# A bias product as a 129th matmul column, a softplus split in two for PE to add, and a new list of steps, in a four-layer graph network kernel

## The chip, the cores and the metric

The kernel runs on one core of one Trainium2 chip. The metric is the device time of one execution in microseconds (us); the median of several runs counts. Profiles come from one further execution, whose own time is given beside its span. Engines: PE multiplies matrices, DVE is VectorE, ACT is ScalarE, POOL is GpSimd, SP issues most transfers.

## What is computed

128 graphs of 64 nodes with 128 features pass through four layers, each of the form x = x + layer(relu(layernorm(x)), adj). The two that the change touches:

```python
# layer 0
g = exp(coeff * (e[..., None] - offsets) ** 2)      # e = adj, 64 offsets
Wf = (ssp(g @ W1.T + b1) @ W2.T + b2) * adj * adj
y = einsum('bjf,bijf->bif', r @ Wa.T, Wf)
y = ssp(y @ Wd1.T + bd1) @ Wd2.T + bd2              # ssp(x) = softplus(x) - log 2
# layer 1 (hyperbolic)
h = proj(mobius_matvec(W, x))                       # uses |x|, |mx| with mx = x @ W.T
h = proj(mobius_add(h, hyp_bias))                   # uses sum(h * hyp_bias) per node
# ... attention over neighbours with silu and a sigmoid, an MLP, expmap, logmap
```

Layer 2 is a convolution with the normalised adjacency, layer 3 a mean of messages. About a quarter of the entries of adj are not zero.

## The kernel before

Eight graphs form a group (NP = 4 pairs; a pair's 128 nodes are the partitions), and there are 16 groups. A node tile is 128 x 4 x 128, that is 128 x 512 values. Neighbours are kept as lists of slots in three blocks (512, 512 and 208 columns), so a neighbour's work comes as tiles of 128 x 1024 or 128 x 512 and their 208-column rests.

Each part of a group's work is a generator called a stream: `load`, `order` (the neighbour lists), `normed_x`, `layer0` with `weights_of`, `squares`, `duo`, `filter_of` and `neighbours`, `layer1_nodes`, `layer1_edges` with `coefs_of`, `rows`, `scores_of` and `heads`, `rest1`, `rest2`, and a few that prepare weights. Each `yield on(engine, ...)` begins a step, which issues a few instructions. The global order is a string written out in full, `ORDER` (492 steps for one iteration). An entry `name@-k` lets that stream of the group k iterations behind do its next step; `name@=k` does a step once, in iteration k. `Weave.run` walks the list for every iteration, so several groups are in flight, and each engine executes its instructions in just the order in which the list issued them. `Weave` also counts the buffers: a step that names a ring takes one of its buffers, `release` gives it back, and `shared(name, 2)` gives it back after two users. In PSUM the ring "big" has three buffers of 128 x 2 x 512 and "sm" two of 128 x 512.

```python
        for name_ in takes:
            used = self.rings[name_][1]
            s.tokens.setdefault(name_, []).append(len(used))
            used.append(False)
```

When a step asks for ACT's other table (`table="log"` or `"silu"`), a table load is issued first (L923); there are five per group in the steady part.

In `layer1_nodes`, layer 0 ends: Wd1 product (L1729 to L1733), ACT copies it with its bias from PSUM (L1737), DVE clamps it at 40 into a second tile (L1740), ACT takes Exp and Ln(1 + .) of that (L1743, L1744), DVE takes the maximum of the two tiles (L1747), and the Wd2 product follows in the helper `pairs_mm` (L1240). Layer 1 begins: x1 (L1755), layernorm (`bn` L1267; `normed` from L1302 on, once per group), transposes (L1233), an ACT copy (L1207), and the linear product, again at L1240. `product_with_bias` multiplies that product by the hyperbolic bias on POOL (L1789) and sums over features on DVE (`reduce_d`, L1259) into `mhb`, four numbers per node row, read at L1690 and L1864.

Other lines that the prediction names. Layer 0, edges: squared weights (L1584, ACT), gaussians (L1600, L1603, ACT), W1 product (L1617) and its Exp and Ln (L1624, L1627), W2 product (L1634) and its product with neighbours (L1639, DVE; L1398 adds halves), the neighbour product (L1663) and ACT's copy (L1669); L1483 scales Wa's product on ACT. Layer 1, edges: spread coefficients (L1385, L1388, L2079, DVE), their products (L2094, L2098, PE), SiLU (L2103, ACT), the score product (L2120, PE), Tanh into a row (L2126, ACT), which goes out and comes back by DMA as th and is put in its place at L2059 (DVE); L2181 follows PE's L2179, and L1319 (`sc`) is a root on ACT. Layer 1, nodes: L1705 to L1719, L1851 to L1868. Layer 2: v (L1282, ACT, the normalised x) enters the adjacency product (L1254, PE, tiles adjT and v); L1433 is the sort key of `order`; L2265, L1287 and L2272 are layer 1's last step on ACT.

Of the kernel before, what the change touches and what calls it, by code (L numbers as in the profile page):

```python
# [20 lines left out]
NP = 4  # L21
GROUPS = B // (2 * NP)
P = 128
# [741 lines left out]
SOFT_MAX = 40.0  # L765
# [10 lines left out]
heads20@-4 turned_from5@=2 heads20@-4 duo00@-2 rest2@-5 layer1_nodes@-3 rest2@-5 filter_of00@-2  # L776
duo02@-2 rest2@-5 product_with_bias@-3 rest2@-5 slots_ranks@=-2 coefs_of12@-4 weights_of12@-2
coefs_of12@-4 product_with_bias@-3 layer1_nodes@-3 coefs_of12@-4 weights2@=3 neighbours00@-2
rest2@-5 filter_of01@-2 turned_from0@=-4 layer1_nodes@-3 duo02@-2 filter_of00@-2 neighbours00@-2
filter_of00@-2 filter_of01@-2 slots_ranks@=0 weights0@=-2 coefs_of20@-4 layer1_nodes@-3  # L780
coefs_of20@-4 layer1_nodes@-3 layer1_edges@-4 layer1_edges@-4 layer1_nodes@-3 layer1_nodes@-3
weights1@=-5 layer1_edges@-4 layer1_nodes@-3 layer1_nodes@-3 rest1@-4 weights2@=3 layer1_nodes@-3
rest1@-4 layer1_nodes@-3 turned_from1@=-2 rest1@-4 layer1_nodes@-3 neighbours01@-2 filter_of02@-2
rest1@-4 filter_of00@-2 layer1_nodes@-3 neighbours01@-2 filter_of02@-2 filter_of01@-2 squares10@-2
layer1_nodes@-3 rest2@-5 layer1_nodes@-3 layer1_nodes@-3 turned_from2@=0 order@-1 layer1_nodes@-3
layer1_nodes@-3 layer1_nodes@-3 layer1_nodes@-3 layer1_nodes@-3 rest1@-4 layer0@-2 layer1_nodes@-3
order@-1 layer1_nodes@-3 layer1_nodes@-3 rest1@-4 layer1_nodes@-3 layer1_nodes@-3 rest2@-5
layer1_nodes@-3 layer1_nodes@-3 layer1_nodes@-3 layer1_nodes@-3 layer1_nodes@-3 layer1_nodes@-3
filter_of00@-2 layer1_nodes@-3 layer1_nodes@-3 layer1_nodes@-3 layer1_nodes@-3 layer1_nodes@-3
turned_from5@=2 layer1_nodes@-3 filter_of00@-2 layer1_nodes@-3 layer1_nodes@-3 norm_of_sum@-3  # L790
neighbours02@-2 duo20@-2 rest2@-5 weights0@=1 filter_of01@-2 rest2@-5 weights0@=1 filter_of00@-2
filter_of00@-2 filter_of01@-2 norm_of_sum@-3 rest2@-5 filter_of02@-2 neighbours02@-2 duo20@-2
layer1_nodes@-3 duo20@-2 rest2@-5 norm_of_sum@-3 layer1_nodes@-3 layer1_nodes@-3 layer1_nodes@-3
order@-1 filter_of01@-2 rest2@-5 filter_of01@-2 weights2@=2 filter_of03@-2 neighbours03@-2
weights2@=2 rest1@-4 layer1_nodes@-3 weights0@=1 filter_of03@-2 neighbours03@-2 rest1@-4
layer1_nodes@-3 filter_of03@-2 layer1_nodes@-3 squares20@-2 filter_of02@-2 order@-1 norm_of_h@-3
x_self@-4 rest2@-5 filter_of02@-2 weights0@=1 filter_of01@-2 norm_of_h@-3 filter_of02@-2
filter_of02@-2 duo22@-2 weights0@=1 layer1_nodes@-3 filter_of20@-2 duo22@-2 layer1_nodes@-3
duo22@-2 filter_of20@-2 layer1_nodes@-3 layer1_nodes@-3 order@-1 layer1_nodes@-3 filter_of02@-2
neighbours20@-2 filter_of22@-2 attention@-3 neighbours20@-2 layer1_nodes@-3 filter_of20@-2  # L800
weights2@=2 layer1_nodes@-3 order@-1 rest2@-5 layer1_nodes@-3 order@-1 layer1_nodes@-3
layer1_nodes@-3 weights0@=1 rest2@-5 attention@-3 filter_of22@-2 layer1_nodes@-3 filter_of22@-2
filter_of03@-2 turned_from1@=-4 filter_of20@-2 order@-1 duo10@-2 one_minus_z@-3 weights0@=0
one_minus_z@-3 rest2@-5 filter_of03@-2 one_minus_z@-3 layer1_nodes@-3 filter_of03@-2
filter_of03@-2 turned_from0@=-2 one_minus_z@-3 layer1_nodes@-3 order@-1 duo10@-2 one_minus_z@-3
rest2@-5 filter_of03@-2 filter_of20@-2 order@-1 filter_of20@-2 layer1_nodes@-3 layer1_nodes@-3
slots_ranks@=-5 layer1_nodes@-3 layer1_nodes@-3 layer1_nodes@-3 layer1_nodes@-3 layer1_nodes@-3
layer1_nodes@-3 layer1_nodes@-3 layer1_nodes@-3 layer1_nodes@-3 layer1_nodes@-3 order@-1
attention@-3 neighbours22@-2 turned_from3@=-2 order@-1 duo10@-2 rest2@-5 attention@-3
neighbours22@-2 order@-1 duo12@-2 weights2@=2 turned_from4@=1 filter_of10@-2 rest2@-5  # L810
filter_of11@-2 duo12@-2 filter_of10@-2 rest2@-5 filter_of10@-2 order@-1 filter_of11@-2
neighbours10@-2 filter_of22@-2 weights0@=-2 rest2@-5 layer1_nodes@-3 rest2@-5 neighbours10@-2
filter_of10@-2 rest2@-5 order@-1 filter_of22@-2 layer1_nodes@-3 filter_of22@-2 filter_of10@-2
duo12@-2 layer1_nodes@-3 rest2@-5 filter_of11@-2 rest2@-5 filter_of12@-2 neighbours11@-2 order@-1
filter_of11@-2 layer1_nodes@-3 layer1_nodes@-3 turned_from3@=-2 layer1_nodes@-3 weights1@=0
filter_of12@-2 neighbours11@-2 filter_of12@-2 squares12@-2 filter_of10@-2 rest2@-5 weights2@=2
filter_of10@-2 layer1_nodes@-3 filter_of10@-2 layer1_edges@-3 coefs_of02@-3 order@-1
filter_of11@-2 order@-1 rest2@-5 filter_of11@-2 coefs_of00@-3 order@-1 rest1@-4 rest2@-5
filter_of13@-2 neighbours12@-2 neighbours13@-2 filter_of13@-2 neighbours12@-2 filter_of13@-2
neighbours13@-2 filter_of12@-2 rows00@-3 filter_of13@-2 turned_from4@=1 order@-1 rest2@-5  # L820
filter_of11@-2 filter_of12@-2 layer0@-2 rows00@-3 filter_of11@-2 filter_of12@-2 filter_of13@-2
filter_of12@-2 filter_of13@-2 filter_of12@-2 rest1@-4 rest1@-4 rows02@-3 scores_of00@-3
scores_of01@-3 rest1@-4 filter_of13@-2 rows02@-3 weights0@=-2 filter_of13@-2 layer0@-2 normed_x@-1
rest1@-4 scores_of00@-3 scores_of01@-3 sums_of_columns@-1 no_scores@-3 product_with_h@-4 rest1@-4
normed_x@-1 normed_x@-1 normed_x@-1 product_with_h@-4 coefs_of10@-3 product_with_h@-4 rest1@-4
scores_of02@-3 heads00@-3 scores_of03@-3 normed_x@-1 rows10@-3 rest1@-4 heads00@-3 normed_x@-1
scores_of02@-3 rest1@-4 rest1@-4 rest1@-4 rest1@-4 rest1@-4 rest1@-4 rest1@-4 rest1@-4 weights1@=1
rest1@-4 rest1@-4 rest1@-4 rest1@-4 order@-1 rest1@-4 rest1@-4 order@-1 coefs_of12@-3 rows10@-3
normed_x@-1 weights0@=-2 layer1_nodes@-2 normed_x@-1 scores_of03@-3 sum_of_both@-4 layer1_nodes@-2
heads02@-3 rows12@-3 scores_of10@-3 scores_of11@-3 rest1@-4 rest1@-4 rest1@-4 coefs_of20@-3  # L830
weights0@=-2 rest1@-4 coefs_of00@-3 rest1@-4 layer1_nodes@-2 rest1@-4 rows12@-3 rest1@-4 rest1@-4
coefs_of00@-3 rest1@-4 rest1@-4 rest1@-4 weights0@=-1 order@-1 rest1@-4 layer1_edges@-3 heads02@-3
layer1_nodes@-2 scores_of10@-3 scores_of11@-3 rest1@-4 layer1_nodes@-2 rest1@-4 order@-1 rest1@-4
order@-1 coefs_of00@-3 layer0@-1 rest1@-4 coefs_of02@-3 rest1@-4 weights_of00@-1 rest1@-4
scores_of12@-3 layer1_nodes@-2 heads10@-3 duo00@-1 weights2@=2 scores_of13@-3 weights0@=-2 load@0
coefs_of02@-3 rest1@-4 layer1_nodes@-2 rest1@-4 coefs_of00@-3 rest1@-4 coefs_of02@-3 rest1@-4
rest1@-4 rest1@-4 layer1_nodes@-2 weights2@=2 rest1@-4 sum_of_both@-4 coefs_of02@-3
weights_of02@-1 scores_of12@-3 heads10@-3 squares00@-1 duo00@-1 scores_of13@-3 weights1@=-3
rest1@-4 rest1@-4 layer1_nodes@-2 rest1@-4 rows22@-3 rows20@-3 turned_from2@=-2 heads12@-3
heads12@-3 squares02@-1 rest1@-4 rows22@-3 layer1_nodes@-2 layer1_nodes@-2 rows20@-3 coefs_of10@-3  # L840
rest1@-4 rest1@-4 coefs_of10@-3 rest1@-4 coefs_of10@-3 rest1@-4 rest2@-4 scores_of22@-3
layer1_nodes@-2 scores_of22@-3 layer1_nodes@-2 norm_of_h1@-2 scores_of20@-3 layer1_nodes@-2
root_of_sums@-4 rest2@-4 layer1_nodes@-2 scores_of20@-3 layer1_nodes@-2 coefs_of12@-3
coefs_of10@-3 weights_of10@-1 weights_of20@-1 rest2@-4 layer1_nodes@-2 weights0@=-1 duo02@-1
"""


def elements(ap):
    n = 1
    for d in ap.shape[1:]:  # L850
        n *= d
    return n


class Stream:
# [92 lines left out]
def sparse_stack(ctx: ExitStack, tc: tile.TileContext, ins, out: bass.AP, flag):  # L948
# [103 lines left out]
    def matrix(name):  # L1052
        return const.tile([P, P], F32, name=name)
# [44 lines left out]
    def weights0():  # L1098
# [19 lines left out]
        yield from turned(raw["Wd1"], wd1T)  # L1118
        w.event("weights0")

    wlinT, attT = matrix("wlinT"), const.tile([P, 2 * P], F32, name="attT")
    m1aT, m1bT, m2T = (matrix(n) for n in ("m1aT", "m1bT", "m2T"))
    hab2, aw2 = (const.tile([P, 1], F32, name=n) for n in ("hab2", "aw2"))
    aw2b = const.tile([P, 32], F32, name="aw2b")
# [1329 lines left out]
```

## Time and profile before

| | before |
|---|---|
| median of 3 runs | 1788.97 us (1787.3 to 1789.33) |
| profiled execution | 1789.83 us, its span 1788.0 us |
| PE busy | 1580.1 us (88%), 10231 instructions |
| DVE busy | 1576.3 us (88%), 4872 |
| ACT busy | 1496.0 us (84%), 2784; of it 92 table loads of 1.28 us |
| POOL busy | 413.3 us (23%), 717 |
| L1302, once per group, starts at | 113.2, 204.3, 301.7, then about every 102 us to 1626.6 |

Busy time counts an engine's own instructions; the span is that of the profiled execution, and its own time is 1.83 us longer. "PEclk" in a window is the TensorE clock that was granted, 1.00 being full speed. In a group's row, "x16" counts instances, then come busy time, mean duration in ns, and the idle time of the engine just before with what ended it. The chain of waits is followed back from the end of a window: each row is a stretch in which the named instructions decided when the next could begin. The product of four small matmuls is listed as x8, since each is issued as two instructions.

### The profile page before, as it was taken

How to read it: one execution, taken by the hardware profiler on the slowest of the kernel's cores; microseconds unless marked ns; L12 is line 12 of the kernel's file. 1: busy time of each engine (PE TensorE's matmuls, PEld its weight loads, DVE VectorE, ACT ScalarE, POOL GpSimd, SP SyncE). 2: the span in 40 equal slices, each digit the busy share in tenths (PEclk: the TensorE clock that was granted, in tenths of full speed). 3: DMA queues.
4: the chain of work that ended last, by engine and by line, in shares of the span. 5: the costliest groups of instructions: out<-in, count | busy, mean ns of one | idle time of the engine just before them, and what ended most of it. 6: DMA issues, size and time to landing. Idle time of an engine off the chain costs nothing.

```text
span 1788.0 us, 30233 instructions
## 1 busy us (share of the span) xinstructions
PE 1580.1 (88%) x10231; PEld 855.9 (48%) x10231; DVE 1576.3 (88%) x4872; ACT 1496.0 (84%) x2784; POOL 413.3 (23%) x717
## 2 busy tenths in 40 slices
PE   3969888998989899898989899898989989896853
PEld 2424444545545455454545454554545455454542
DVE  5659799999999999999999999999999999988853
ACT  2858898989899898989899898989989898986632
POOL 1010113123221413223121312322141322302221
PEclk8979999999999999999999999999999999997865
DMA  2000202011110202011020201111020201102110
GB/s 62 6 1 7 57 7 54 11 43 24 27 46 16 58 7 57 17 34 34 16 58 10 60 10 38 30 27 46 16 58 1 50 18 29 36 7 58 33 37 9
DMA packets 57173, 54.22 MB, mean 30 GB/s; under 512 B 13616, under 2 KB 40624, under 8 KB 57008
## 3 DMA queue, kind: packets, MB, share of 16 engines
q1 hardware_dynamic: 57008, 52.19, 11.8%
q8 instruction: 83, 1.36, 0.3%
q14 instruction: 82, 0.67, 0.1%
HBM read 7.61 MB, written 4.19 MB: 7 GB/s over the span
## 4 chain that ended last, share of the span: by engine, by line
PE 48%; ACT 30%; DVE 14%; issue 3%; POOL 2%; DMA 2%; SPq 1%; DVEq 0%; ACTq 0%; POOLq 0%
PE big L1634 7%; PE sm L1240 7%; PE big L2094 6%; PE big L2076 5%; PE big L1617 5%; PE big L1663 4%; ACT ex L1624 4%; PE sm L2120 3%; ACT ex L1627 3%; PE big L2098 3%; ACT e L1600 3%; DVE ex L1639 2%; ACT ra L1669 2%; ACT e L1603 2%; PE sm L1247 2%
## 5 line engine op out<-in xcount | busy, mean ns | idle before, releaser
L1634 PE MATMUL big<-ex,w2T 128*128 128x512 f32 (+1 forms) x768 | 296.5, 519 | 10.4 <-DVE den L1707 5.6
L1639 DVE SCALAR_TENSOR_TENSOR ex<-big,c_L_gnn_b,ra 128x1024 f32<-128x1024 f32 (+1 forms) x160 | 198.4, 1240 | 28.4 <-PE big L1634 27.0
L1617 PE MATMUL big<-e,w1T 64*128 64x512 f32 (+1 forms) x768 | 187.2, 581 | 10.9 <-ACT e L1603 8.3
L1634 PEld LDWEIGHTS big<-ex,w2T 128*128 128x128 f32 x768 | 134.2, 190 | 122.2 <-issue 72.5
L1624 ACT ACTIVATE ex<-big,c_L_gnn_b 128x1024 f32<-128x1024 f32 (+1 forms) x160 | 174.5, 1091 | 7.4 <-PE big L1617 6.9
L2094 PE MATMUL big<-va,U 64*128 64x512 f32 (+1 forms) x768 | 175.3, 532 | 4.9 <-DVE va L2079 4.9
L1663 PE MATMUL big<-va,a 64*128 64x512 f32 (+1 forms) x768 | 176.8, 560 | 2.9 <-ACT va L1584 1.8
L2103 ACT ACTIVATE ex<-big,c_L_gnn_att_b 128x1024 f32<-128x1024 f32 (+1 forms) x160 | 167.6, 1078 | 9.8 <-PE big L2098 9.4
L2098 PE MATMUL big<-slot_r,Sx 64*128 64x512 f32 (+1 forms) x768 | 165.9, 507 | 0.0
L1627 ACT ACTIVATE ex<-ex 128x1024 f32<-128x1024 f32 (+1 forms) x160 | 165.4, 1033 | 0.1
L1669 ACT ACTIVATE ra<-big 128x1024 f32<-128x1024 f32 (+1 forms) x160 | 160.2, 1001 | 3.5 <-PE big L1663 1.7
L1398 DVE TENSOR_TENSOR ex<-ex 128x512 f32<-128x512 f32 (+1 forms) x256 | 140.4, 554 | 1.4
L2214 POOL TENSOR_TENSOR w<-w,hh 128x512 f32<-128x512 f32 x16 | 22.1, 1379 | 454.7 <-DVE w L2206 441.6
L923 ACT ACT_TABLE_LOAD x92 | 118.0, 1283 | 2.2 <-PEq L2442 0.7
L2059 DVE COPY_PREDICATED att<-oh,th 128x256 f32<-128x256 uint16 x256 | 111.4, 446 | 8.2 <-DMA th<-row 8.0
L2076 PE MATMUL big<-oh,pqs 64*64 64x512 bf16 (+1 forms) x1152 | 115.0, 337 | 0.0
L1663 PEld LDWEIGHTS big<-va,a 64*128 64x128 f32 x768 | 73.2, 198 | 87.1 <-issue 47.1
L2079 DVE COPY_PREDICATED va<-slot_r,big 128x1024 f32<-128x1024 uint32 (+1 forms) x96 | 105.2, 1097 | 5.7 <-PE big L2076 5.5
L2120 PE MATMUL sm<-ex,aw2b 128*32 128x512 f32 (+1 forms) x640 | 98.0, 593 | 11.0 <-ACT ex L2103 11.0
L2098 PEld LDWEIGHTS big<-slot_r,Sx 64*128 64x128 f32 x768 | 73.6, 187 | 59.9 <-issue 59.9
L1254 PE MATMUL big<-adjT,v 64*128 64x64 f32 x256 | 31.5, 424 | 74.5 <-ACT v L1282 74.5
L1617 PEld LDWEIGHTS big<-e,w1T 64*128 64x128 f32 x768 | 65.4, 197 | 63.9 <-issue 28.6
(570 smaller groups left out, 3678.0 us busy)
## 6 DMA issues: line engine op xcount, KB each, us to landing
th<-row SPq DMA_DIRECT2D x128, 256.0 KB, 3.5
th<-row SPq DMA_DIRECT2D x64, 104.0 KB, 2.2
x<-in_x_dram SPq DMA_DIRECT2D x16, 256.0 KB, 2.8
out_dram<-v SPq DMA_DIRECT2D x16, 256.0 KB, 2.3
adj<-in_adj_dram SPq DMA_DIRECT2D x16, 128.0 KB, 2.4
e<-in_L_gnn_att_w_dram SPq DMA_DIRECT2D x2, 64.0 KB, 4.4
bR<-in_L_gnn_mlp_w_dram SPq DMA_DIRECT2D x2, 64.0 KB, 3.6
wupd<-in_L_gnn_W_upd_dram SPq DMA_DIRECT2D x1, 128.0 KB, 3.4
```

The lines of the kernel that those rows point to most:

```text
L1617: T.matmul(dst, lhsT=w1T[HALF[h], :], rhs=e[HALF[h], b, 0:W], start=True, stop=True)
L1624: act(ex[:, :, 0:wide], pre[:, :, 0:wide], AF.Exp, bias=b1)
L1627: act(ex[:, :, 0:wide], ex[:, :, 0:wide], AF.Ln, bias=1.0)
L1634: T.matmul(wf[:, b, cols], lhsT=w2T, rhs=ex[:, b if c < 2 else b ^ j, cols], start=True, stop=True)
L1639: V.scalar_tensor_tensor(two.rearrange("q (j r) -> q j r", j=2), wf[:, :, 0:wide], b2s, ra[:, :, 0:wide], ALU.add, ALU.mult)
L1663: T.matmul(nb[:, b, at * W:at * W + W], lhsT=rf[rows, p + j, :], rhs=factors[0][rows, k + j, :], start=True, stop=True)
L1669: act(ra[:, :, 0:wide], nb[:, :, 0:wide], AF.Copy)
L2076: T.matmul(rk[h, k, 0:W], lhsT=pqs[h, s, p, :], rhs=oh[h, p, at:at + W], start=s == 0, stop=s == 2)
L2094: T.matmul(pre[:, b, col], lhsT=U[h, p + k, :], rhs=coefs[h, k, :], start=True, stop=False)
L2098: T.matmul(pre[:, b, col], lhsT=Sx[s][h, p + k, :], rhs=slot_r[h, at:at + W], start=False, stop=s == 1)
L2103: act(a[:, :, 0:wide], pre[:, :, 0:wide], AF.Silu, bias=ab1)
L2120: T.matmul(sl[here, 0:wide], lhsT=aw2b, rhs=a[:, b, 0:wide], start=True, stop=True)
```

## The change

Softplus is written as relu(x) + log(1 + exp(-|x|)). ACT makes both relu and the absolute value from PSUM, Exp and Ln run on the second, and the two tiles are not joined on DVE: the Wd2 product takes each in turn and adds them up in PSUM (eight matmuls in place of four). The clamp and the maximum on DVE go.

The weights of the linear product get a 129th column, W^T times the hyperbolic bias, made once by a new stream `bias_column` on DVE. So the product itself yields `mhb` as the last column of each block; DVE copies these four columns out of PSUM, in place of a product on POOL and a sum on DVE. 4 x 129 columns no longer fit a bank, so this product moves from the ring "sm" to "big", and is given back when both ACT's copy and DVE's copy are done.

The list of steps has 490 entries in place of 492, and much of it stands in another order. The group offsets of steps and the transfers that they issue are the same but for where one iteration is cut off. Seen engine by engine, in one period: on DVE, the copy of `mhb` comes after five L1388 and two L2059; L1851 and L1433 come before L2181; one L1398 comes after `sc`; L1639 comes three places earlier at one place, and L2309 ahead of L1388. On ACT, L1584 comes before the last L2126 and L1600 after L2265. The table loads stay at the same places.

```diff
@@ -762,7 +762,6 @@
 SLOTS = sum(WIDTHS)
 RC = max(r + n for _, r, n, _ in BLOCKS[2])
 STEPS = [(42, 1.0), (34, 2.0), (21, 2.0), (11, 4.0), (2, 6.0)]
-SOFT_MAX = 40.0
 SERIES_A = float(np.sqrt(0.2))
 SERIES_B = 1.0 / (6.0 * SERIES_A)
 SERIES_REST = 1.0 - SERIES_B * SERIES_B
@@ -773,75 +772,76 @@
 
 PE, DVE, ACT, POOL = "PE", "DVE", "ACT", "POOL"
-heads20@-4 turned_from5@=2 heads20@-4 duo00@-2 rest2@-5 layer1_nodes@-3 rest2@-5 filter_of00@-2
...
+rest2@-5 layer1_nodes@-3 filter_of01@-2 weights2@=3 neighbours00@-2 rest2@-5 weights0@=-1
...
@@ -1118,7 +1118,8 @@
         yield from turned(raw["Wd1"], wd1T)
         w.event("weights0")
 
-    wlinT, attT = matrix("wlinT"), const.tile([P, 2 * P], F32, name="attT")
+    wlinx, attT = const.tile([P, P + 1], F32, name="wlinx"), const.tile([P, 2 * P], F32, name="attT")
+    wlinT = wlinx[:, 0:P]
     m1aT, m1bT, m2T = (matrix(n) for n in ("m1aT", "m1bT", "m2T"))
     hab2, aw2 = (const.tile([P, 1], F32, name=n) for n in ("hab2", "aw2"))
     aw2b = const.tile([P, 32], F32, name="aw2b")
@@ -1158,6 +1159,15 @@
         V.tensor_tensor(hb2, hb, hb, ALU.mult)
         V.tensor_reduce(hby2, hb2, AX.X, ALU.add)
         w.event("bias1")
+        w.add(bias_column())
+
+    def bias_column():
+
+        yield on(DVE, after=[("weights1",), ("bias1",)])
+        prod = raw_tile()
+        V.tensor_tensor(prod, wlinT, hb, ALU.mult)
+        V.tensor_reduce(wlinx[:, P:P + 1], prod, AX.X, ALU.add)
+        w.event("wlinx")
 
     turns = []
 
@@ -1734,21 +1744,21 @@
                      start=False, stop=b == 1)
         w.release("ys", st["ys_used"])
         yield on(ACT)
-        act(flat(spn), pre, AF.Identity, bias=bd1)
+        act(flat(spn), pre, AF.Relu, bias=bd1)
+        act(flat(ex), pre, AF.Abs, bias=bd1)
         w.release("sm")
-        yield on(DVE)
-        V.tensor_scalar(ex, spn, SOFT_MAX, None, ALU.min)
         w.event("soft_ready", g)
         yield on(ACT, table="log")
-        act(ex, ex, AF.Exp)
+        act(ex, ex, AF.Exp, scale=-1.0)
         act(ex, ex, AF.Ln, bias=1.0)
         w.event("soft", g)
-        yield on(DVE)
-        V.tensor_tensor(spn, spn, ex, ALU.max)
+        yield on(PE, "sm")
+        pt = bank()
+        for p in range(NP):
+            for k, part_ in enumerate((spn, ex)):
+                T.matmul(pt[:, p, :], lhsT=part_[:, p, :], rhs=wd2T, start=k == 0, stop=k == 1)
+        w.release("a0")
         w.release("a1")
-        yield on(PE, "sm")
-        pt = pairs_mm(spn, lambda p: wd2T)
-        w.release("a0")
         yield on(DVE, "x1")
         x1 = st["x1"] = pers.tile([P, NP, D], F32, name="x1", tag="x1", bufs=3)
         st["x1_used"] = w.token("x1")
@@ -1778,25 +1788,30 @@
         evac(hT, pt)
         w.release("sm")
 
-        yield on(PE, "sm")
-        pt = pairs_mm(hT, lambda p: wlinT)
+        yield on(PE, "big", after=[("wlinx",)])
+        pt = big()
+        for p in range(NP):
+            T.matmul(pt[:, p // 2, p % 2 * (P + 1):(p % 2 + 1) * (P + 1)], lhsT=hT[:, p, :],
+                     rhs=wlinx, start=True, stop=True)
+        pt = pt[:, :, 0:2 * (P + 1)].rearrange("q b (a d) -> q b a d", a=2)
+
+        def product_with_bias():
+            yield on(DVE)
+            V.tensor_copy(mhb.rearrange("q (b a) -> q b a", b=2), pt[:, :, :, P])
+            used()
+            w.event("mhb", g)
+
+        used = w.shared("big", 2)
+        w.add(product_with_bias())
         yield on(ACT)
-        evac(mx, pt)
-        w.release("sm")
-
-        def product_with_bias():
-            yield on(POOL, after=[("n2", g), ("bias1",)])
-            G.tensor_tensor(tmp, mx, bm(hb, NP), ALU.mult)
-            yield on(DVE)
-            reduce_d(mhb, tmp)
-            w.event("mhb", g)
+        evac(mx.rearrange("q (b a) d -> q b a d", b=2), pt[:, :, :, 0:P])
+        used()
 
         yield on(ACT, after=[("n2", g)])
         squares_sum(n2[:, 1], h1, mx)
         yield on(DVE)
         nn, rr = ttile("nn", 2, NP), ttile("rr", 2, NP)
         V.tensor_scalar(nn, n2, MIN_NORM2, None, ALU.max)
-        w.add(product_with_bias())
         yield on(ACT, table="log")
         act(nn, nn, AF.Ln)
         act(rr, nn, AF.Exp, scale=-0.5)
```

## The prediction

> **What bounds the kernel now.** I read the page first: busy shares and the chain that ended last.
>
> ```profile
> PE 1580.1 (88%) x10231; PEld 855.9 (48%) x10231; DVE 1576.3 (88%) x4872; ACT 1496.0 (84%) x2784; POOL 413.3 (23%) x717
> PE 48%; ACT 30%; DVE 14%; issue 3%; POOL 2%; DMA 2%; SPq 1%; DVEq 0%; ACTq 0%; POOLq 0%
> ```
>
> PE, DVE and ACT are within five points of each other, POOL is free, and the chain passes from engine to engine. So relief of one engine counts only where the chain lies on it. I then followed the chain of waits through one group (716 to 830 us). From one L1254 product (721.14) to the next (823.66) it lies on PE for 10.6 us, on DVE from 731.76 to 739.34, on ACT to 764.66, on PE without a gap to 807.03, and mostly on ACT to 823.66:
>
> ```profile
> 804.24 1.09 PE sm L1240 x8
> 805.33 1.70 PE sm L2120 x8
> 807.03 0.02 issue
> 807.05 0.69 ACT row L2126
> ...
> 822.16 1.06 ACT e L1603
> 823.22 0.40 ACT v L1282
> 823.61 0.04 issue
> 823.66 1.97 PE big L1254 x16
> ```
>
> The first row is the Wd2 product that the change doubles: it is on the path. Then I read PE's timeline before L1254, and the windows around what follows:
>
> ```profile
> 716.73 0.91 PE L2120 MATMUL sm<-ex,aw2b 128*32 128x416 f32 x8 [0.51 <-ACT ex L2103]
> 721.14 1.98 PE L1254 MATMUL big<-adjT,v 64*128 64x64 f32 x16 [3.50 <-ACT v L1282]
> ```
>
> ```profile
> core 0: us, PE busy (x) PEld busy (x) DVE busy (x) ACT busy (x) POOL busy (x), PEclk, DMA share, GB/s
> 516.22:523.05 6.83, 6.42 (x28) 3.88 (x29) 6.50 (x22) 6.73 (x16) 1.27 (x1) 0.50 0.15 32
> 523.05:618.62 95.57, 89.88 (x612) 48.22 (x610) 90.68 (x281) 86.60 (x160) 24.65 (x42) 1.00 0.13 32
> 618.62:625.45 6.83, 6.42 (x28) 3.88 (x29) 6.50 (x22) 6.73 (x16) 1.26 (x1) 0.50 0.15 32
> ```
>
> Once per group PE idles 3.50 us for ACT (rows, a table load, L1603, v), and the granted clock then drops to half for 6.83 us. The drops between 311.42 and 1540.22 are 102.40 us apart every time, as if on a raster, though L1254 itself starts 0 to 1.64 us after the drop. How the next group went depends on that offset. The distance between starts of L1302 (one per group) was 101.78 us at an offset of 1.64, 101.95 at 0.64, 102.1 at 0.2, and 102.5 or more near 0. A late start puts less PE work under the slow clock and makes the next group shorter; an early one makes it longer. So the group's length is held at 102.40 as long as the work needs between about 101.8 and 102.6 us. Twelve of the fifteen distances lie in this regime; three at the beginning (91.1, 97.5, 101.8) and the tail from 1626 us do not.
>
> **The Trainium skill beside this.** "TensorE: Matmul & The Clock Gate" (section "What's actually happening") says that the clock falls after an idle window of 3413 ns and comes back after one busy one, and that the windows run free of the kernel. The raster agrees: 102.40 us is 30 such windows. The release does not: here it took 6.83 us. By one window, a slow stretch would cost half; the sum below uses the rows alone.
>
> **The change, part by part** (per group; the durations are means over 16 instances).
>
> ```profile
> L1737 ACT ACTIVATE a<-sm,c_L_gnn_bd 128x512 f32<-128x512 f32 x16 | 11.2, 698 | 4.5 <-issue 2.7 <-PE sm L1733 1.6
> L1740 DVE TENSOR_SCALAR a<-a 128x512 f32<-128x512 f32 x16 | 6.7, 419 | 11.6 <-ACT a L1737 11.6
> L1747 DVE TENSOR_TENSOR a<-a,a 128x512 f32<-128x512 f32 x16 | 11.0, 684 | 1.3 <-ACT a L1744 1.2 <-issue 0.2
> L1259 DVE TENSOR_REDUCE mhb<-n 128x4 f32<-128x512 f32 x16 | 10.8, 677 | 0.0
> L1789 POOL TENSOR_TENSOR n<-n,r_L_gnn_b_lin 128x512 f32<-128x512 f32 x16 | 22.2, 1387 | 13.8 <-ACT n L1207 13.8
> ```
>
> DVE loses 0.42 + 0.68 + 0.68 and gains a 128x4 copy from PSUM. No row is that copy; a 128x4 DVE operation takes 0.16 (L1864), so about 1.6 us of 102 go, 26 us in all. POOL loses 1.39. ACT gains an Abs pass over the same PSUM tile; bound below by the 128x512 Exp at 0.63 and above by its twin at 0.70; I take 0.70. PE gains four matmuls: two such products in one chain row took 1.78 us (766.65, x16), so 0.89. The 129th column adds 1/128 to one product: 0.01, dropped.
>
> What of it is on the path: *PE* +0.89, entirely, since the doubled product stands in the gapless stretch just ahead of L2120. *DVE*: nothing directly. L1740 and L1747 (697.8 and 700.6) and the reduce run while the chain is on PE, and in the one DVE stretch of the chain there is none of them. The waits for them in the table, 11.6 and 1.3 us, come from three instances near the start, not from the steady part. *ACT*: the Abs stands where ACT waited 0.96 us for PE (L1483) shortly before, and the product that needs its result starts only after 701.9, while Ln ends at 700.2: covered by over 1 us of slack. Without that cover it costs 0.70. Relu and Abs add no table load: the changed list keeps five per group, at the same places. *POOL*: the product was waited for by nobody; nothing.
>
> The new order of steps gives some back. On DVE, L1851 and the key L1433 move ahead of L2181 in the chain's stretch and a 0.34 us L1398 behind sc: about -0.4. On ACT, va (L1584) moves before the last L2126, filling its wait for PE, and L1600 moves behind L2265; against a new wait of some 0.65 for L2098 this is -0.3. L1639 comes three places earlier and may remove a 0.33 us PE gap, which I count at nothing. The 3.50 us gap keeps its ACT steps, so the half clock stays. SP's list of x, adj and th transfers stays in order.
>
> One resource is new: the linear product takes a "big" PSUM buffer instead of "sm", held until ACT's copy and DVE's 128x4 copy are both done. That copy is queued behind five L1388 and two L2059; it would run about 722.5 and the L1617 product that needs the buffer comes at about 723.6. So DVE's new wait for PE is already over, and 1 us of slack covers the hold.
>
> Sum: 0.89 - 0.4 - 0.3 = about +0.2 us per group. Ends: +0.89 if the order gives nothing; -0.5 if it also removes PE's 0.33 gap and the 0.35 wait before L2094 for a DVE copy. Added to 101.8 to 102.6 this stays inside what 102.40 can hold, so the twelve held groups cost nothing and the four others 4 x 0.2 = 0.8. In the first group the softplus path is one of latency: out go 0.42 + 0.68, in come 0.70 + 0.89, about +0.5 before hand-overs; the one-time product for the column (128x128, two small DVE steps) is under 0.7, the price of the 128x512 reduce. Start and tail (113 and 162 us) are reordered as well, which I can price only as +-4, taking 0. The profiled execution was 1789.83 (span 1788.0 and 1.83 around it), 0.86 above the median: 1789.83 + 0.8 + 0.5 = 1791.1, less 0.86 is 1790.3; I say **1790**.
>
> **Rivals.**
> *B, slower: the doubled product is not repaid.* PE +0.89 with the order giving nothing back. It decides once the work needs over 102.4 us even at the best offset: 101.78 + 0.89 = 102.67 does. Then at least 12 x 0.27 + 4 x 0.89 = 6.8, at most 15 x 0.89 = 13.4: 1796 to 1803, say **1799**. For it: the product stands in a gapless PE stretch. Against: the moved DVE and ACT steps stand on the chain too.
> *C, faster: the raster lets go downward.* If DVE's 1.6 us brings more than -0.4 per group, L1254 starts before the raster point, the idle stretch falls partly into the earlier window, and the half clock lasts one window, as at 168.06 and 215.85 (3.4 us each). One window is 6.83 / 2 = 3.41 us, and at half clock it holds half its work, so 1.7 us are saved; but the next start is then 1.7 nearer to an earlier raster point, so every second group: 12 x 0.85 = 10, **1779**, with 1776 to 1785 around it. For it: DVE is 88% busy and the removed steps free its queue ahead of every later one. Against: no steady-state wait names them.
> *D: the buffer held too long.* If the copy is later than 1 us, L1617 and the ACT pass behind it wait; price and side as in B, and it is counted there.
>
> **Chances.** Held by the raster (forecast) 0.50, with its own range 1785 to 1796: of that 0.31 falls within 0.2% (3.6 us, about what a measurement of this kernel can tell from no change), 0.11 slower, 0.08 faster, by start and tail. B with D 0.30, all slower. C 0.20, all faster. So faster 0.28, same 0.31, slower 0.41. For the range I leave out the far half of C and the top of B: 1778 to 1803.
>
> **What would show it.** Right: L1254 to L1254 still 102.40 us in the middle, half clock for 6.83 us once per group, L1240 of Wd2 at about 1.95 us, the gap before L1254 near 3.5, DVE near 1551 us busy, PE near 1594. Wrong upward: spacing of 102.7 or more, or a wait before L1617 that ends at the copy mhb. Wrong downward: half clock of 3.4 us in many groups or a spacing below 102. The forecast would also be wrong if the start, where steps wait for single results, moved by more than 4 us.

## The result, and the profile after

| | before | changed |
|---|---|---|
| median | 1788.51 us (8 runs, 1787.30 to 1790.07) | 1794.22 us (8 runs, 1793.25 to 1795.60) |
| profiled execution | 1789.83, span 1788.0 | 1794.83, span 1793.0 |

The ratio is 1.003, 95% interval 1.0021 to 1.004: slower by some 5.7 us. The median lies in the range, on the side that was given most chance (slower, 0.41), and 4.2 us above the forecast. But 0.30 of that 0.41 belonged to rival B, which is not what happened; a group length that is held and a time that is clearly longer had been given 0.11. The busy times moved as the parts of the change say (page of the changed kernel):

```profile
PE 1588.2 (89%) x10359; PEld 867.3 (48%) x10359; DVE 1546.2 (86%) x4842; ACT 1501.9 (84%) x2800; POOL 406.6 (23%) x701
PE 48%; ACT 25%; DVE 19%; issue 3%; POOL 2%; DMA 1%; SPq 1%; DVEq 0%; ACTq 0%; POOLq 0%
```

DVE lost 30 us, POOL 7, PE gained 8, ACT 6, and the kernel is slower: no engine's sum sets the time. The groups by line give the prices of the new work, Wd2 now being 256 instructions, and Abs 0.70 us:

```profile
L1759 PE MATMUL sm<-wd2T,a 128*128 128x128 f32 x256 | 34.5, 290 | 2.2 <-ACT a L1753 1.4 <-ACT a L1747 0.8
L1748 ACT ACTIVATE a<-sm,c_L_gnn_bd 128x512 f32<-128x512 f32 x16 | 11.2, 702 | 0.0
```

PE's timeline and the windows show that the half clock stayed. First come the product before the gap and L1264 (the L1254 of before), with PE's idle time in brackets; then windows of time, PE's clock being the third figure from the end:

```profile
722.55 0.91 PE L2135 MATMUL sm<-ex,aw2b 128*32 128x416 f32 x8 [1.06 <-ACT ex L2118]
726.96 1.97 PE L1264 MATMUL big<-adjT,v 64*128 64x64 f32 x16 [3.51 <-ACT v L1292]
```

```profile
726.09:732.92 6.83, 5.96 (x26) 3.56 (x28) 6.27 (x22) 6.73 (x17) 1.26 (x1) 0.50 0.23 46
732.92:828.49 95.57, 90.76 (x622) 49.24 (x618) 89.20 (x279) 87.07 (x160) 23.71 (x41) 1.00 0.13 32
828.49:835.32 6.83, 6.05 (x26) 3.56 (x28) 6.26 (x21) 6.73 (x17) 1.26 (x1) 0.50 0.22 45
```

The drops of the clock from 316.49 to 1556.08 us are again 102.40 us apart, without exception. Where the 5.0 us between the two profiled spans lie is read from the starts of the layernorm subtraction, once per group (L1302 before, L1312 after):

| stretch | before | changed | difference |
|---|---|---|---|
| start to group 1 | 113.16 | 114.49 | +1.33 |
| group 1 to 3 | 188.58 | 192.44 | +3.86 |
| group 3 to 15 | 1227.11 | 1227.93 | +0.82 |
| group 15 to the end | 259.19 | 258.18 | -1.01 |

Twelve groups together cost 0.8 us; the first two cost 3.9. The first row is mostly chance: six profiles below that keep the old list and the old softplus have 110.5 to 115.5 us there.

### The profile page after: what moved, and what is told of

It is laid out like the page before. It is cut to its first block, busy times and chain, and to the rows that moved or that the text cites. A ratio compares the mean times of both kernels' runs of the same rounds, so it can differ in the third digit from the quotient of the medians.

```text
span 1793.0 us, 30484 instructions
## 1 busy us (share of the span) xinstructions
PE 1588.2 (89%) x10359; PEld 867.3 (48%) x10359; DVE 1546.2 (86%) x4842; ACT 1501.9 (84%) x2800; POOL 406.6 (23%) x701
## 4 chain that ended last, share of the span: by engine, by line
PE 48%; ACT 25%; DVE 19%; issue 3%; POOL 2%; DMA 1%; SPq 1%; DVEq 0%; ACTq 0%; POOLq 0%
PE big L1644 8%; PE big L2109 6%; PE big L1627 5%; PE sm L1250 5%; PE big L2091 4%; PE big L1673 4%; ACT ex L1634 3%; PE big L2113 3%; DVE ex L1649 3%; PE sm L2135 2%; PE big L1264 2%; ACT ex L2118 2%; PE sm L1257 2%; ACT ex L1637 2%; ACT n L1297 2%
## 5 line engine op out<-in xcount | busy, mean ns | idle before, releaser
L1627 PE MATMUL big<-e,w1T 64*128 64x512 f32 (+1 forms) x768 | 195.7, 612 | 10.4 <-ACT e L1613 7.7
L1673 PE MATMUL big<-va,a 64*128 64x512 f32 (+1 forms) x768 | 167.0, 531 | 1.9 <-DVE ex L1649 1.2
L2135 PE MATMUL sm<-ex,aw2b 128*32 128x512 f32 (+1 forms) x640 | 91.4, 589 | 17.8 <-ACT ex L2118 17.8
L1627 PEld LDWEIGHTS big<-e,w1T 64*128 64x128 f32 x768 | 69.0, 208 | 69.1 <-issue 18.5
L1264 PE MATMUL big<-adjT,v 64*128 64x64 f32 x256 | 31.6, 424 | 72.3 <-ACT v L1292 72.3
```

The costliest lines, as they stand in the source:

```text
L1627: T.matmul(dst, lhsT=w1T[HALF[h], :], rhs=e[HALF[h], b, 0:W], start=True, stop=True)
L1673: T.matmul(nb[:, b, at * W:at * W + W], lhsT=rf[rows, p + j, :], rhs=factors[0][rows, k + j, :], start=True, stop=True)
```

## The experiments

The kernels with the old list keep the order of what is left on each engine as it was before, so each isolates its edit. "Distance" is the median of the twelve distances from one L1302 to the next between groups 3 and 15.

**The softplus alone, in the old list.** The diff's softplus; of the old list, the two steps of `layer1_nodes` that DVE lost are taken out.

> The old list and the old bias product; only the softplus is the new one (Relu and Abs on ACT, eight Wd2 matmuls, no DVE clamp and maximum). Every engine's order is that of before. Theory R (the raster of the clock holds the group's length): L1254 to L1254 stays 102.40 us in the middle, and the time moves by no more than the start costs, 1787 to 1792 us. Theory S (every group pays its price): 0.89 us of PE per group, 1788.5 + 15 x 0.89 = 1802 us.

Measured: 1796.57 us (5 runs), ratio 1.004 (1.0027 to 1.0054). Neither figure: half of what theory S asks for. The middle grew by 5.0 us, and not evenly: most distances are 102.0 to 103.0, but one is 104.3 and one 103.9; there L1254's place against the drops moved from 0.94 us after one to 0.87 us ahead of one, with 105.81 us between these two drops, and two half clocks (1239.35 and 1341.75) lasted 3.41 us. The long distances go with a transfer: in them DVE waited 2.7 and 2.3 us at L2059 for th, against about 1.1 in most other groups. With the clock kept up (below) a distance of 104.1 stands in the place of the first, again with 2.7 us of that wait, so the clock did not make that one. Why the transfer was late there was not looked into.

**The 129th column alone, in the old list.** To let "big" be free in the list's account, one block of steps (`slots_ranks` to `product_with_bias`) stands ahead of `filter_of00@-2`.

> The old list (one block of it stands a few entries earlier, each engine's order is kept) and the old softplus; only the bias product is the 129th column. Theory R and theory S alike: 1788.5 +- 2, since DVE's sum and POOL's product were on nobody's path. If the copy mhb holds the big buffer too long, L1617 waits in every group, 0.5 to 1 us each, and the distance of L1254 grows unless the raster holds it.

Measured: 1789.21 us (11 runs), ratio 1.0001 (0.9992 to 1.001). As expected; the copy costs 0.15 us and the buffer is back in time.

**Both parts, in the old list.**

> Both parts of the change, but in the old list of steps. If the code costs the time that was lost at the start (5.2 us up to the third group), this is at 1793 to 1796 like the changed kernel; if the new list costs it, 1788 to 1791. By theory S, without what the new list gives back: 1800 or more.

Measured: 1793.03 us (11 runs), ratio 1.0019 (1.0009 to 1.0028). The total falls at the edge of the first case, but not for its reason: groups 1 to 3 took 190.02 us, so of the 3.86 lost there the code costs 1.4 and the new list 2.4. The middle is 2.7 us longer than before's, where the changed list had 0.8.

**The Wd2 product issued twice, in the kernel before.**

```diff
         pt = pairs_mm(spn, lambda p: wd2T)
+        for p in range(NP):
+            T.matmul(pt[:, p, :], lhsT=spn[:, p, :], rhs=wd2T, start=True, stop=True)
```

> The kernel before, with the Wd2 product issued twice (the same four matmuls again, 0.89 us of PE per group, nothing taken away anywhere). Theory R: the middle groups stay at 102.40 us, L1254 settles later against the drop of the clock, and the time is 1788 to 1792. Theory S: 15 x 0.89 = 13.4 more, 1802.

Measured: 1793.53 us (11 runs), ratio 1.0024 (1.0015 to 1.0033). That lies outside both ranges: of 13.4 us only 4.6 arrive. The middle grew by 1.75 us, with the drops 102.40 us apart. That alone doesn't tell whether the raster swallowed the price or whether it was never on the path. The next three do.

**The clock kept up.** Seven matmuls whose result is overwritten fill PE's gap ahead of L1254:

```diff
-    def by_graph(lhsT, rhs):
+    def by_graph(lhsT, rhs, warm=0):
 
         pt, n = big(), rhs.shape[-1]
+        for _ in range(warm):
+            T.matmul(pt[:, 0, 0:256], lhsT=ident, rhs=attT[:, 0:256], start=True, stop=True)
...
-        pt = by_graph(hs, adjT)
+        pt = by_graph(hs, adjT, warm=7)
```

> The kernel before, with seven 128x256 matmuls of the identity (0.43 us each, estimated from the 0.86 us of a 128x512 one, 3.0 us in all) put into the buffer of the L1254 product ahead of it, in the 3.50 us in which PE waits for v; the product then overwrites them. Theory R: the clock doesn't drop in the middle, the 102.40 us spacing ends, and each group gains up to 3.4 us (half of 6.83 us at half speed): 1789 - 15 x (1 to 3.4) = 1738 to 1774. Theory S (the spacing is just the sum of the work, and the slow clock is hidden behind ACT and DVE): 1787 to 1791.

> The changed kernel with the same seven matmuls. Theory R: as fast as the kernel before with them, plus the price per group that the raster hid: by the prediction's sum +0.2 us x 15 = +3, by the bare doubled product +13; and if DVE binds now, up to 24 less. Theory S: 1793 to 1796, as without them.

> The kernel with the Wd2 product issued twice, and the same seven matmuls. Theory R: with no raster to hold the group's length, the 0.89 us show in full: +10 to +14 against the kernel before with the seven matmuls (without them it was +4.6). Theory S: the same +4.6 as without them.

Measured: 1783.47 us (9 runs; 0.997, 0.996 to 0.998), 1785.41 (10 runs; 0.998, 0.9971 to 0.999) and 1786.86 (10 runs; 0.9986, 0.9976 to 0.9995). The same 400 us of the kernel before, without and with the seven matmuls:

```profile
700.00:1100.00 400.00, 375.61 (x2493) 203.56 (x2490) 379.08 (x1169) 364.82 (x681) 98.35 (x163) 0.97 0.13 31
700.00:1100.00 400.00, 383.07 (x2569) 207.43 (x2566) 381.02 (x1182) 366.62 (x683) 99.16 (x163) 1.00 0.13 32
```

With the clock at 1.00 the 102.40 is gone. The distances, free of the raster, are 101.77 before, 101.64 changed, 101.87 with Wd2 twice. So the raster exists and did hold the groups, but both guesses of size were wrong. A group gains 0.46 us from a full clock (102.23 to 101.77; 0.63 against the 102.40 of the drops), not 1 to 3.4. And the doubled product costs 0.1 us per group when nothing holds the group's length, not 0.89: the raster did not swallow its price, it was hardly on the path. Where the +3.4 us between the medians of these two lie is not shown: the two profiled spans differ by 1.6, and the stretch to group 1, which varies by chance, by 2.4 (115.51 against 113.14).

**Where the 0.89 went.** The chain of waits of three kernels at the Wd2 product: before, with Wd2 twice, and with the new softplus, each with the seven matmuls and the old list.

```profile
702.27 1.09 PE sm L1240 x8
703.35 1.71 PE sm L2122 x8
705.09 0.69 ACT row L2128
```

```profile
703.97 1.09 PE sm L1240 x8
705.06 0.89 PE sm L1754 x8
705.95 1.04 PE sm L2124 x8
707.01 0.69 ACT row L2130
```

```profile
701.30 1.98 PE sm L1751 x16
703.29 1.39 PE sm L2122 x8
704.70 0.69 ACT row L2128
```

The score product (L2120 in the kernel before) takes 1.04 us when it doesn't wait. Before it took 1.71: in the middle of the row it waited for ACT's SiLU. The waits of PE's weight loads in the kernel before say so (700 to 710 us; total, times, longest):

```profile
PEld sm L2120 <- ACT ex L2103: 0.6, 1, 0.6
```

So four more matmuls before it mostly fill this wait. In the third chain the row is still 1.39, and a wait is listed again (698 to 710 us):

```profile
PEld sm L2122 <- ACT ex L2105: 0.2, 1, 0.2
```

The last of these SiLU passes ends 3.31 us after the Wd2 product begins, against 2.73 in the two other kernels (medians of ten groups). So with the new softplus this SiLU sets the end of the row, and the doubled product hides under it: 1.98 + 1.39 is 0.57 more than 1.09 + 1.71. ACT and PE were nearly level here, and the Abs pass (0.70 us) stands on ACT ahead of the SiLU, where ACT had no room. A kernel with the Abs pass alone was not run.

**The softplus and both parts, and the column alone, with the clock kept up.**

> The new softplus alone in the old list (which gave 1796.6), with the seven matmuls that keep the clock up. If its 7.6 us come from slipping past points of the raster (one distance of 104.3 and one of 103.9 in its profile), they shrink to what the groups pay freely: 1783.5 + 15 x 0.1 to 0.3 + the start's 1.5, so 1786 to 1790. If ACT's added Abs pass or the doubled product costs it in each group, the distance of L1254 is 102.2 or more and the time 1791 or more.

> Both parts of the change in the old list, with the seven matmuls. Against the changed kernel with them (1785.4): if the new list costs 2.4 us at the start and gives 0.1 per group back, this is at 1784 to 1786 with a middle distance of 101.7 to 101.8; if the new list is what makes the middle shorter, 1787 or more.

> The 129th column alone in the old list, with the seven matmuls. DVE's sum (0.68 us) and POOL's product go and nothing is added on PE: middle distance 101.5 to 101.75, time 1780 to 1784, not slower than the kernel before with the seven matmuls (1783.5).

Measured: 1792.66 us (10 runs; 1.0021, 1.0012 to 1.0031), 1791.79 (10 runs; 1.0008, 0.9999 to 1.0018) and 1782.06 (5 runs; 0.9963, 0.9948 to 0.9977). The softplus went the way of its second case (each group pays, 102.24), both parts in the old list that of theirs (it is the new list that makes the middle shorter), and the column came as expected. Put beside the others:

| kernel | median, as is | distance | median, clock kept up | free distance |
|---|---|---|---|---|
| before | 1788.9 | 102.23 | 1783.5 | 101.77 |
| + column | 1789.2 | 102.31 | 1782.1 | 101.69 |
| + softplus | 1796.6 | 102.43 | 1792.7 | 102.24 |
| + both, old list | 1793.0 | 102.44 | 1791.8 | 102.26 |
| + both, new list (the change) | 1794.2 | 102.34 | 1785.4 | 101.64 |
| + Wd2 twice | 1793.5 | 102.37 | 1786.9 | 101.87 |

In the free column the parts add up to within 0.1 us: softplus +0.47 per group, the column -0.08, the new list -0.62. Of the softplus' 0.47 the doubled product has 0.10 by the run with Wd2 twice, which leaves some 0.37 for the Abs pass by subtraction. DVE's relief of 1.1 us by the softplus bought nothing that shows: over the twelve groups DVE now waits 16.4 us for the transfer th, where the kernel before waited 2.2 (both with the clock kept up; the softplus first):

```profile
DVE att L2061 <- DMA th<-row: 16.4, 14, 2.7
```

```profile
DVE att L2061 <- DMA th<-row: 2.2, 3, 1.1
```

In the column of distances as they are, six kernels lie within 0.21 us. The new list gives 6.4 us when the clock is kept up (1791.8 to 1785.4). Under the raster it gives nothing that could be told (1793.0 against 1794.2), because most of its gain per group is lost to the 102.40 (in the profiles its middle is only 1.9 us shorter, 1227.93 against 1229.78) while its price in the first two groups stays.

**The price of the new list at the start.** Group 1 to 3 took 190.0 us in both kernels with the new code and the old list, 192.4 and 193.8 with the new list. PE's idle time from group 1 to 2 is 9.8 us and 13.2 (12.6 with the clock kept up). Three waits of that stretch (113 to 210 us) in the changed kernel:

```profile
PE sm L1243 <- DVE hh L1273: 2.2, 1, 2.2
ACT e L1610 <- PE big L1605: 3.6, 1, 3.6
ACT ex L1634 <- DVE y L1408: 2.5, 3, 1.4
```

The first was 1.4 before, the other two are not among the longer waits before. From group 1 to 2 the chain of waits lies on PE for 45.9 us with the new code and the old list and for 23.8 with the new list, on ACT for 7.1 and 23.7. A reason that fits, but was not tested: in a list laid out for several groups in flight, these steps follow others which the only two groups at hand haven't reached. Which entries of the list do it was not tried.

**The column alone, with the clock kept up to the end.** A helper puts 2 to 8 such matmuls ahead of products that wait in groups 13 to 15, and 36 ahead of the last L1254.

> As the run before, and in the last three groups more such matmuls ahead of products that wait (2 to 8 of 0.43 us each, 36 ahead of the last L1254, where PE idles 19.4 us). After 1627 us PE has some 90 us of work at a mean clock of 0.70; if it stays at 1.00 and half of what is gained lies on the chain, 5 to 12 us less: 1770 to 1779. If matmuls overrun their gaps or the chain is on the other engines: 1780 to 1786.

Measured: 1775.31 us (4 runs; 0.992, 0.9904 to 0.9937), as expected in the first case. The windows from 1626 to 1775 us, without and with them:

```profile
1626.00:1775.00 149.00, 91.78 (x599) 63.28 (x597) 86.82 (x352) 60.85 (x156) 34.41 (x62) 0.75 0.10 25
1626.00:1775.00 149.00, 114.80 (x741) 80.09 (x741) 88.61 (x360) 63.36 (x166) 36.02 (x65) 0.93 0.11 27
```

From group 15 to the end it is 252.87 us instead of 259.44. This is the fastest version of the study.

**The changed kernel with all of that.**

> The changed kernel with all the added matmuls of the run with the 129th column alone (1775.3), the same numbers in the same places. From the profiles without the tail's matmuls: the first two groups +4 to +5 us, the middle -0.05 x 12 = -0.6, the end 0 to -3: 1776 to 1779 us. If the changed list's shorter groups count for more once nothing rounds them up, it is at 1775 or less.

Measured: 1777.37 us (5 runs; 0.9931, 0.9918 to 0.9945), as worked out: groups 1 to 3 took 192.3 us against 188.7, and the middle didn't make up for it.

## Why the prediction was right or wrong, point by point

*The raster holds the middle: right.* Drops 102.40 us apart, the half clock 6.83 us, the gap 3.51: all as named, and 0.8 us for twelve groups. It was also put to the test: with the gap filled, the one distance became six, from 101.64 to 102.26, each kernel its own. But the rows that the prediction set against the offset were a choice: three groups with distances of 102.5 to 102.8 had L1254 at 0.81 to 1.30 us after the drop. In these PE idled 4.15 to 4.42 us in place of 3.50, and DVE waited 0.9 to 1.1 us for th, so the offset alone does not give a group's length.

*PE +0.89, entirely on the path: wrong.* Measured +0.10. I took the row "1.70 PE sm L2120 x8" for work, though the same product took 1.06 elsewhere in that chain. The 0.6 us between them was a wait for ACT, listed among the waits of the weight loads.

*The Abs pass covered: wrong.* About +0.37 per group, by subtraction (softplus 0.47 less 0.10). I looked at Ln's end against the Wd2 product, which had room, and not at what stands behind on ACT: the three SiLU passes for which that same L2120 waited.

*The new list gives 0.7 back: nearly right.* Measured 0.62 in the free distance. So the sum, +0.2, against -0.13 measured, came out near by luck: two errors cancel in part, too much for PE and nothing for ACT.

*The start at +0.5 and +-4: too low.* Groups 1 to 3 cost 3.9, 1.4 by the code and 2.4 by the list. I priced the softplus' latency and left the order of steps to the margin. This term carries most of the miss of 4.2 us. With the 1.3 us up to group 1, which vary by chance, the start moved by 5.2 us, more than the 4 that the prediction itself named as a sign of being wrong.

*Rival B* (the product is not repaid, 1796 to 1803) did not occur by its mechanism; the softplus alone comes to 1796.6, through ACT. *Rival C* did not occur in the changed kernel either: of DVE's 1.6 us the column's part bought 0.1 per group, and the softplus' part (1.1 us) shows as a longer wait for th. The half clock of one window that it named did come in two groups of the softplus alone, which took 101.97 and 102.24 us: 0.2 to 0.4 less than 102.40, and not 1.7. *Rival D*: the copy took 0.15 us and was waited for once, 0.5 us, in 16 groups.

*The rule of the Trainium skill*: "TensorE: Matmul & The Clock Gate", section "What's actually happening", gives the release as after one busy window or more; the prediction took it as one. In the middle the half clock lasted 6.83 us in nearly all groups, even where this product began 0.2 to 0.3 us ahead of the drop (the column alone) and PE was busy for all of the first window. It lasted 3.41 us where L1254 began 0.87 and 1.03 us ahead (the softplus alone). The two windows after a drop, the column alone first (PE's busy time is the second figure, its clock the third from the end):

```profile
1231.13:1234.54 3.41, 3.41 (x22) 2.28 (x22) 1.91 (x3) 3.31 (x12) 1.27 (x1) 0.50 0.17 35
1234.54:1237.95 3.41, 3.41 (x14) 1.91 (x10) 3.38 (x20) 3.41 (x5) 0.00 (x0) 0.50 0.00 0
```

```profile
1239.35:1242.76 3.41, 3.41 (x14) 1.84 (x16) 3.12 (x7) 3.31 (x11) 1.27 (x1) 0.50 0.04 8
1242.76:1246.17 3.41, 3.41 (x20) 1.85 (x18) 3.38 (x21) 3.41 (x5) 0.00 (x0) 1.00 0.00 0
```

So one busy window was enough in one case and not in the other; what decides is open.

## What to carry to other kernels

A row in a chain of waits can hold a wait: compare its duration with the same operation's elsewhere before calling it work, and read the weight loads' waits too. Where a loop's period is a multiple of a clock's window, price an edit by what is left free of it, because gains and losses per turn can both mostly vanish while what happens before the first locked turn is paid in full. And filling a regular idle gap of PE with matmuls that nobody reads was worth more here (0.3% in the kernel before; 0.8% with the tail and the 129th column) than the whole change.

## What the runs showed of the hardware that was not expected

The half clock followed a stretch in which PE was idle for only 2.37 of the 3.41 us ahead of the drop (311.42 in the kernel before: L1254 began 1.64 us after it, with 3.50 us idle ahead of that), so PE needn't be idle throughout. In the filled kernel a drop (519.57) even followed 3.41 us with 1.17 idle, while 1.48 idle (from 936.00 on) was followed by none; idle time alone does not decide it. The raster stands elsewhere against the kernel's start in each execution: the drops, counted modulo 3.413 us, were at 0.81, 2.46, 0.31, 2.34, 0.95 and 1.53 in six profiles. That this makes the spread of 2 to 3 us between runs of one kernel fits, but was only argued.
